# A graph-attention kernel: in the last pass, every fourth step sums A (E - 1) g into the bank of the A f products

## The chip, the cores and the metric

The kernel runs on one core of one Trainium2 chip. The metric is the device time of one execution in microseconds (us); the time of a version is the median of its runs.

## The reference, cut to what matters

Two layers work on 4096 nodes with 512 features. Layer 0 is graph attention with 8 heads of width 64, followed by a residual sum and a layer norm. Layer 1 is attention inside graphs of 128 nodes, again with residual and layer norm.

```python
# layer 0, per head h; A is the 4096 x 4096 adjacency of zeros and ones
feats   = einsum('nf,hfo->hno', X, W)
dense   = s_self[:, :, None] + s_neigh[:, None, :]
dense   = where(dense > 0, dense, 0.2 * dense) * A    # a missing edge counts with exp(0) = 1
out     = softmax(dense) @ feats ; relu ; x = layernorm(x + out)
# layer 1
scores  = (x Wq^T)(x Wk^T)^T * scale + 2 adj, inside blocks of 128 ; off-block scores are -1e6 * (2 adj)
x       = layernorm(x + (softmax(scores) * mask) @ (x Wv^T))
```

A missing edge has the weight 1 and an edge the weight E = exp(leaky(s + t)), where s belongs to the row's node and t to the neighbour. So a row of layer 0 is the sum of all f (S), plus the sum over edges of (E - 1) f, divided by the sum of the weights.

## The kernel before, in words

**How E is taken apart.** With p = exp(0.8 s), u = exp(-0.2 s), d = exp(-0.8 t) and g = exp(t) f, the product u E f is max(p, d) g. So u times the wanted sum is u (S - A f) + A max(p, d) g. The kernel keeps two PSUM accumulators of two banks each: `accf` sums -A f and `acc` sums A max(p, d) g. At the end of a chunk `sums_to_rows` forms `y = (accf + S) * u_row + acc` (L1259 and L1267).

**Tiling.** A pass r (0 to 3) treats two heads. A pass has four chunks c of 1024 target nodes, and a chunk has 32 steps j of 128 neighbours. For one step VectorE makes two tiles of 128 x 1024 called `q`, one per head (L1475): `q = max(p_row, d) * A`. ScalarE turns q into a `mark` of zeros and ones for the denominators (L1485); of each fourth step, the second head's mark is made on VectorE (L1480). TensorE does 4 matmuls `accf` with the adjacency tile `at` and the two halves of f (L1499), and 8 matmuls `acc` with q and g (L1521), each on 32 columns; in the trace each of the 8 appears as two. Every eight steps the `dens` matmuls sum the marks (L1536).

**Order of the work.** In the last pass four steps form a group, so a chunk has the groups g0 to g7. TensorE runs in the order of the program: in a group 16 accf, then pieces of other work, then 32 acc (64 in the trace), then further pieces. The other engines are ordered by the framework's scheduler. In the last pass the pool of q tiles has 6 buffers, that is three steps: the q of a fourth step can be written only when acc of the first step of its group has been read. `at` has 6 buffers too, and is loaded on the SP queue.

**The pieces.** In the chunks c1, c2 and c3 of the last pass, the lists `PLAN` and `PLANS` put layer 1 of the preceding chunk between the main matmuls. A chunk is two blocks of layer 1, "a" and "b". "E" closes the preceding chunk: transposes of the denominators and of `y` into three PSUM tiles `ps_m` (L1316, L1339), and on VectorE `parts`, `rd` (L1319 to L1332) and two multiplications `hst` (L1340), which free the PSUM tiles. Then `rows_of_layer_0` makes the rows `x1b` (L1246), and a layer norm follows. The pieces a and b transpose x1b (L1075), make scores (L1095, L1122, L1131), values (L1167, L1175) and output rows (L1181, L1183). In c1, block b does not exist yet; in c2 and c3, block b of the chunk before is finished in g0 to g2. All these pieces take their PSUM tiles from the same three buffers in turn (`misc`).

**The setup** ends with the rows of exponentials: `exponentials` writes p and u of 128 nodes to `pu_j` (L744), `rows_of_exponentials` transposes them on TensorE (L768), copies them on ScalarE (L777) and stores them to the DRAM tensor `pu_d`, from which p_row and u_row are later loaded as broadcast rows (L1412, L1418).

Of the kernel before, what the change touches and what calls it, by code (L numbers as in the profile page):

```python
# [404 lines left out]
def adjacency_streamed_path(  # L405
# [55 lines left out]

    g_d = dram.tile([PR, NT // 4, P, 4 * FP], F32, name="g_d")
    f_d = dram.tile([PR, NT // 4, P, 4 * 2 * FP], F32, name="f_d")
    pu_d = dram.tile([2 * H, N], F32, name="pu_d")
    at_d = dram.tile([NCH, NT, P, C], F32, name="at_d")
    hs_d = dram.tile([N, FP * (PR - 1)], F32, name="hs_d")

# [25 lines left out]
    p_all, u_all = pu_all[:, :, 0, :], pu_all[:, :, 1, :]  # L493
    n0 = const.tile([P, NT], F32, name="n0")
    nb_all = const.tile([P, NT, H], F32, name="nb_all")
    e_all = early.tile([P, NT, 2, H], F32, name="e_all")
    e_b = const.tile([P, NT, H, 6], BF16, name="e_b")

# [36 lines left out]
    urowp = ctx.enter_context(tc.tile_pool(name="urows", bufs=1))  # L535
    evp = ctx.enter_context(tc.tile_pool(name="ev", bufs=1))
    hp_ = ctx.enter_context(tc.tile_pool(name="hout", bufs=1))
    ckp = ctx.enter_context(tc.tile_pool(name="ck", bufs=2))
    ps0 = ctx.enter_context(tc.tile_pool(name="ps_misc", bufs=1, space=PSUM))
    banks = [ps0]  # L540

# [90 lines left out]
    with tc.tile_pool(name="setup1", bufs=1, side="right") as one, tc.tile_pool(  # L632
# [97 lines left out]
        def exponentials(k, u, sc):  # L730

            j = 4 * k + u
            if u == 0:
                pu_js[k] = two.tile([P, 4, 2, H], F32, name="pu_j")
            st = small.tile([P, 5, H], F32, name="st")
            for lo, hi, w in ((0, 3, 1), (3, 5, 0)):
                ends_of_setup["DVE", u] = nc.vector.tensor_tensor(
                    st[:, lo:hi].rearrange("p k (q h) -> p k q h", q=2),
                    sc[:, None, :, :, w].to_broadcast([P, hi - lo, 2, H // 2]),
                    powers[:, lo:hi].rearrange("p k (q h) -> p k q h", q=2),  # L740
                    OP.mult,
                )
            nc.scalar.activation(e_all[:, j], st[:, 0:2], AF.Exp)
            nc.scalar.activation(pu_js[k][:, u], st[:, 3:5], AF.Exp)  # L744
            nc.scalar.activation(d_all[:, j, :], st[:, 2], AF.Exp)

        def parts_of_exponentials(k):
            blk = slice(4 * k, 4 * k + 4)
            nc.vector.tensor_scalar_mul(
                nb_all[:, blk, :], d_all[:, blk, :], -BIG * (1.0 + 2.0**-23)  # L750
            )
            eb = e_b[:, blk]
            for i in range(2):
                src = e_all[:, blk, i, :]
                rest = small.tile([P, 4, H], F32, name="rest")
                nc.vector.tensor_copy(eb[:, :, :, 3 * i], src)
                nc.vector.tensor_sub(rest, src, eb[:, :, :, 3 * i])
                nc.vector.tensor_copy(eb[:, :, :, 3 * i + 1], rest)
                nc.vector.tensor_sub(eb[:, :, :, 3 * i + 2], rest, eb[:, :, :, 3 * i + 1])
            nc.vector.tensor_copy(  # L760
                e_p[:, blk, :NE].rearrange("p j (m h) -> p j h m", h=H), eb[:, :, :, :3]
            )
            nc.vector.tensor_scalar_mul(eb[:, :, :, :3], eb[:, :, :, :3], -1.0)

        def rows_of_exponentials(k):
            pr = pss.tile([2 * H, 4, P], F32, name="ps_set")
            for u in range(4):
                nc.tensor.transpose(  # L768
                    pr[:, u, :], pu_js[k][:, u].rearrange("p k h -> p (k h)"), ident
                )  # L770
            if k < NB - 1:
                row = late.tile([2 * H, 4 * P], F32, name="pu_row")
            else:
                row = hp_.tile([P, CT, FP], F32, name="hst")
                row = row.rearrange("p t n -> p (t n)")[: 2 * H, : 4 * P]
            rows[k] = row
            ends_of_setup["ROW"] = nc.scalar.copy(  # L777
                row.rearrange("p (q n k) -> p q k n", q=2, k=2),
                pr.rearrange("p (q k) n -> p q k n", q=2),
            )  # L780
            nc.gpsimd.dma_start(pu_d[:, ts(k, 4 * P)], row)

        def columns_of_exponentials(k, pc=None):
            pc = pss.tile([P, 4, 2 * H], F32, name="ps_set") if pc is None else pc
            for u in range(4):
                nc.tensor.transpose(pc[:, u, :], rows[k][:, ts(u, P)], ident[: 2 * H, : 2 * H])
            nc.vector.tensor_copy(
                pu_all[:, 4 * k : 4 * k + 4].rearrange("p u k h -> p u (k h)"), pc
            )
# [138 lines left out]
    def columns_of_last():  # L928

        columns_of_exponentials(NB - 1, misc([P, 4, 2 * H]))  # L930

    psa = ctx.enter_context(tc.tile_pool(name="ps_acc_f", bufs=1, space=PSUM))
    dens = psa.tile([P, HB], F32, name="dens")
    nc.vector.memset(dens, 0.0)
# [134 lines left out]
    def layer_1(blk, x1b, lp, lp1, lp2):  # L1069
# [45 lines left out]
            if c % 2:  # L1115
                yield
        pq = misc([P, 4, P])
        ns = lp1.tile([P, 4, P], F32, name="ns")
        nm = small.tile([P, 4], F32, name="nm_f")
        for u in range(4):  # L1120
            for f in range(FC):
# [72 lines left out]
        pp = misc([P, 4, P])  # L1194
        for u in range(4):
            nc.tensor.transpose(pp[:, u, :], ns[:, u, :], ident)
        pT = lp1.tile([P, 4, P], F32, name="pT_f")
        nc.scalar.copy(pT, pp)
        values(1)
        yield  # L1200
# [49 lines left out]
    def sums_to_rows(r, c, acc, accf, ae, u_row, later_by):  # L1250
# [25 lines left out]
        def pieces():  # L1276
# [55 lines left out]
            nc.vector.reciprocal(rd, rd)  # L1332
            if r == 0:
                yield later_by
            hst = hp_.tile([P, CT, FP], F32, name="hst")
            for t4 in range(0, CT, 4):
                fin = misc([P, 4, FP])
                for t in range(4):
# [65 lines left out]
    def main_pass(r, ae=None, wide=4):  # L1404

        for c in range(NCH):
# [8 lines left out]
            for h in range(2):  # L1415
                in_order(
                    r == 0 and c < 2,
                    nc.sync.dma_start(  # L1418
                        u_row[h * FH : (h + 1) * FH, :],
                        broadcast_rows(pu_d[H + 2 * r + h, ts(c, C)], FH, C),  # L1420
                    ),
                )
            def pieces(c, group, place):
                if r == PR - 1 and c:
                    run_plan(PLANS[c == NCH - 1][group][place])
                elif place == (r == 0):
                    run_pieces((0.75 if r else 1.0) * wide)
# [18 lines left out]
            for j0 in range(0, NT, wide):  # L1446
# [13 lines left out]
                    in_order(r == 0 and c == 0 and j0 < 16, ins)  # L1460
                if at_step == 0:
                    cast_steps(0, 6, last_pair)
                follow = [
                    x
                    for x in steps[at_step + wide : at_step + 2 * wide]
# [3 lines left out]
                for j in cycle:  # L1469
                    for h in range(2):  # L1470
                        hh = 2 * r + h
                        q = qs[j, h] = ring("q", qp, 6).tile([P, C], F32, name="q")
                        d_j = d_all[:, j, hh : hh + 1]
                        with following(at_step == 0, ("DVE", 3 if j else 2)):
                            ends_of_setup["Q"] = nc.vector.scalar_tensor_tensor(  # L1475
                                q, p_row[h], d_j, ats[r, c, j].bitcast(F32), op0=OP.max, op1=OP.mult
                            )
# [16 lines left out]
                    with following(True, "Q"):  # L1494
                        parts_of_exponentials(NT // 4 - 1)
                for j in cycle:
                    for w in range(2):
                        for s in range(2):
                            nc.tensor.matmul(  # L1499
                                accf[:, s, :],  # L1500
                                f_s[j // 4][:, j % 4, w, :],
                                ats[r, c, j][:, ts(s, HB)],
                                start=(j == 0 and w == 0),
                                stop=(j == NT - 1 and w == 1),
                            )
# [9 lines left out]
                    pieces(c, j0 // 4, 0)  # L1515

                for j in cycle:
                    for s in range(2):
                        for o in range(0, FP, 32):
                            h = o // FH  # L1520
                            nc.tensor.matmul(  # L1521
                                acc[o : o + 32, s, :],
                                g_s[j // 4][:, j % 4, h, o % FH : o % FH + 32],
                                qs[j, h][:, ts(s, HB)],
                                start=(j == 0),
                                stop=(j == NT - 1),
                            )
                if r == 0:
                    pieces(c, j0 // 4, 1)
# [117 lines left out]
```

## Time and profile before

| | us |
|---|---|
| median of 3 runs | 2055.48 (2055.07 to 2056.7) |
| profiled execution | 2057.91, its span 2056.1 |
| chunks c0, c1, c2, c3 of the last pass, from the first accf matmul of each | 1354.1, 1450.8, 1604.8, 1775.3 |
| last acc matmul of the last pass ends | 1931.9 |

The profiled execution is one of its own; its time lies 2.4 us above the median of the runs. In the profile PE is TensorE, PEld its weight loads, DVE VectorE, ACT ScalarE, POOL GpSimd and SP the queue that issues most loads. "busy" of TensorE is modelled: a busy TensorE can still be held up by a late operand. In a line of a group, the shapes follow as output and input, then the count, the busy time in us and the mean in ns, and behind the bar the idle time before it and who ended it.

### The profile page before, as it was taken

How to read it: one execution, taken by the hardware profiler on the slowest of the kernel's cores; microseconds unless marked ns; L12 is line 12 of the kernel's file. 1: busy time of each engine (PE TensorE's matmuls, PEld its weight loads, DVE VectorE, ACT ScalarE, POOL GpSimd, SP SyncE). 2: the span in 40 equal slices, each digit the busy share in tenths (PEclk: the TensorE clock that was granted, in tenths of full speed). 3: DMA queues.
4: the chain of work that ended last, by engine and by line, in shares of the span. 5: the costliest groups of instructions: out<-in, count | busy, mean ns of one | idle time of the engine just before them, and what ended most of it. 6: DMA issues, size and time to landing. Idle time of an engine off the chain costs nothing.

```text
span 2056.1 us, 38302 instructions
## 1 busy us (share of the span) xinstructions
PE 2030.4 (99%) x15105; PEld 1051.0 (51%) x15105; DVE 1671.9 (81%) x2125; ACT 1542.2 (75%) x1878; POOL 224.2 (11%) x361
## 2 busy tenths in 40 slices
PE   9999999999999999999999999999999999999997
PEld 7884555555544444444454444544454445545453
DVE  5668888888899998798998999999975984896654
ACT  3349888888879889788898989998885666567420
POOL 1222222222100000000000000000210210210111
PEclk9999999999999999999999999999999999999999
DMA  6999999999999999798999999989974764775211
GB/s 208 245 325 259 287 288 276 291 268 289 271 373 337 354 352 335 257 310 298 319 323 340 316 336 323 326 295 358 323 237 144 250 242 137 225 274 169 73 49 43
DMA packets 207371, 551.31 MB, mean 268 GB/s; under 512 B 24780, under 2 KB 65740, under 8 KB 207180
## 3 DMA queue, kind: packets, MB, share of 16 engines
q1 hardware_dynamic: 142828, 426.31, 59.6%
q0 software_dynamic: 62272, 121.91, 23.2%
q8 instruction: 121, 1.98, 0.4%
q10 hardware_dynamic: 2080, 0.52, 0.1%
q14 instruction: 70, 0.57, 0.1%
HBM read 491.79 MB, written 107.22 MB: 291 GB/s over the span
## 4 chain that ended last, share of the span: by engine, by line
PE 93%; DVE 4%; issue 1%; DMA 1%; SPq 0%; POOL 0%; ACT 0%; POOLq 0%; DVEq 0%
PE acc L1521 41%; PE accf L1499 23%; PE ps_fe L800 5%; PE ps_m L1167 5%; PE dens L1536 5%; PE ps_m L1095 5%; DVE q L1475 3%; PE ps_m L1122 1%; PE ps_m L610 1%; PE ps_m L1181 1%; PE ps_m L1075 1%; PE ps_m L1024 1%; PE ps_m L1339 1%; PE ps_set L720 1%; PE ae L1435 1%
## 5 line engine op out<-in xcount | busy, mean ns | idle before, releaser
L1475 DVE SCALAR_TENSOR_TENSOR q<-p_row,d_all,at 128x1024 f32<-128x1024 f32 x1024 | 1242.0, 1277 | 146.9 <-PE acc L1521 121.1
L1485 ACT ACTIVATE mark<-q,nb_all 128x1024 fp8e4<-128x1024 f32 x896 | 995.5, 1145 | 184.3 <-DVE q L1475 168.6
L1521 PE MATMUL acc<-q,g_s 128*32 128x512 f32 x8192 | 903.4, 593 | 1.1 <-DVE q L1475 0.4
L1521 PEld LDWEIGHTS acc<-q,g_s 128*32 128x32 f32 x8192 | 264.1, 110 | 594.4 <-issue 533.0
L1499 PE MATMUL accf<-at,f_s 128*128 128x512 f32 x2048 | 495.2, 398 | 2.1 <-ACT at L621 2.1
L1499 PEld LDWEIGHTS accf<-at,f_s 128*128 128x128 f32 x2048 | 380.3, 188 | 110.4 <-issue 26.4
L1230 ACT ACTIVATE ck<-ck,neg_half_f 128x1024 f32<-128x1024 f32 x128 | 146.0, 1141 | 25.5 <-DMA ck<-in_adj_dram 25.4
L1231 ACT ACTIVATE ck<-ck,neg_quarter 128x1024 f32<-128x1024 f32 x128 | 146.3, 1143 | 1.7
L1536 PE MATMUL dens<-mark,e_b 128*6 128x512 fp8e4 x2048 | 125.3, 379 | 0.0
L800 PE MATMUL ps_fe<-w_sb_f,xT_f 128*128 128x264 f32 (+1 forms) x512 | 121.1, 393 | 1.9 <-ACT xT_f L723 1.9
L621 ACT CAST at<-ps_m 128x1024 fp32r<-128x1024 fp8e4 x124 | 116.4, 1025 | 4.8 <-PE ps_m L610 4.3
L1167 PE MATMUL ps_m<-wvT,x1T 128*128 128x512 f32 x256 | 114.2, 594 | 0.0
L1095 PE MATMUL ps_m<-x1T,M_sb 128*128 128x512 f32 x256 | 112.9, 594 | 0.0
L800 PEld LDWEIGHTS ps_fe<-w_sb_f,xT_f 128*128 128x128 f32 x512 | 100.1, 199 | 16.4 <-ACT xT_f L723 2.5
L1350 POOL DMA_DIRECT2D hs_d<-hst x12 | 10.7, 896 | 847.8 <-DVE hst L1340 847.8
L1480 DVE TENSOR_SCALAR mark<-q,d_all 128x1024 fp8e4<-128x1024 f32 x128 | 96.3, 752 | 4.7
L622 POOL DMA_DIRECT2D at_d<-at x128 | 69.0, 541 | 272.3 <-ACT at L621 248.1
L1536 PEld LDWEIGHTS <-e_b 128*6 128x6 bf16 x2048 | 54.7, 86 | 77.7 <-issue 34.6
L1095 PEld LDWEIGHTS ps_m<-x1T,M_sb 128*128 128x128 f32 x256 | 48.0, 190 | 59.3 <-issue 58.4
L1167 PEld LDWEIGHTS ps_m<-wvT,x1T 128*128 128x128 f32 x256 | 47.6, 190 | 56.4 <-issue 55.2
L1175 DVE TENSOR_TENSOR v_t<-ps_m,bv_row 128x512 f32<-128x512 f32 x32 | 21.7, 684 | 60.5 <-PE ps_m L1167 60.5
L1102 ACT ACTIVATE zT<-ps_m,zb 128x512 f32<-128x512 f32 x32 | 21.7, 680 | 61.2 <-PE ps_m L1095 61.2
(195 smaller groups left out, 1099.5 us busy)
## 6 DMA issues: line engine op xcount, KB each, us to landing
at<-at_d SPq DMA_DIRECT2D x384, 512.0 KB, 6.3
f_s<-f_d SPq DMA_DIRECT2D x128, 512.0 KB, 7.8
at_d<-at POOLq DMA_DIRECT2D x128, 512.0 KB, 14.8
ck<-in_adj_dram SPq DMA_DIRECT2D x128, 512.0 KB, 5.5
g_s<-g_d SPq DMA_DIRECT2D x128, 256.0 KB, 5.6
f_d<-fst POOLq DMA_DIRECT2D x16, 1024.0 KB, 7.9
a_b<-in_adj_dram POOLq DMA_DIRECT2D x32, 512.0 KB, 17.4
p_row<-pu_d SPq DMA_DIRECT2D x32, 512.0 KB, 6.9
```

Source lines behind the costliest of these rows:

```text
L621: ends_of_setup["ACT"] = nc.scalar.copy(at, both[:, :, k])
L800: nc.tensor.matmul(pf[:, q, :, cols], tile_j(xTs[k][:, c].rearrange("p u n -> p (u n)"), u), w_sb[:, c, 4 * q : 4 * q + 4, cols], start=(c ...
L1095: nc.tensor.matmul(pz, L1["M"][:, f, ts(c, P)], x1T[:, f, :], start=(f == 0), stop=(f == FC - 1),)
L1167: nc.tensor.matmul(pv, x1T[:, f, ts(u, P)], L1["wvT"][:, f, :], start=(f == 0), stop=(f == FC - 1),)
L1230: tc.keep_in_program_order(nc.scalar.activation(ck, ck, AF.Square, bias=neg_half))
L1231: nc.scalar.activation(ck, ck, AF.Abs, bias=neg_quarter, accum_out=binp[:, k : k + 1])
L1475: ends_of_setup["Q"] = nc.vector.scalar_tensor_tensor(q, p_row[h], d_j, ats[r, c, j].bitcast(F32), op0=OP.max, op1=OP.mult)
L1480: nc.vector.tensor_scalar(mark, q, d_j, None, op0=OP.is_gt, saturate=False)
L1485: nc.scalar.activation(mark, q, AF.Sigmoid, bias=nb_all[:, j, hh : hh + 1], scale=BIG, saturate=False,)
L1499: nc.tensor.matmul(accf[:, s, :], f_s[j // 4][:, j % 4, w, :], ats[r, c, j][:, ts(s, HB)], start=(j == 0 and w == 0), stop=(j == NT - 1 an ...
L1521: nc.tensor.matmul(acc[o : o + 32, s, :], g_s[j // 4][:, j % 4, h, o % FH : o % FH + 32], qs[j, h][:, ts(s, HB)], start=(j == 0), stop=(j ...
L1536: nc.tensor.matmul(dens[lo : lo + 6, :], e_b[:, j, 2 * r + h, :], marks[j, h][:, ts(s, HB)], start=(j == 0), stop=(j == NT - 1),)
```

## The change

In chunks c1, c2 and c3 of the last pass, the steps j = 2, 6, ..., 26 are folded: one step in each of the groups g0 to g6, 21 steps in all. A folded step has no accf matmuls. Its q is made by two VectorE instructions per head in place of one, `max(p_row, d) * U_row` and then `(q - c) * A`, with U = 1/u as a broadcast row and c = exp(-t) as a column. So q g is A (E - 1) f, and its 8 matmuls add to accf in place of acc. Its mark is made on ScalarE from the sign of q, with a constant bias (a folded step never is the one whose mark VectorE makes).

To have U and c, the setup takes reciprocals: eight of 128 x 8 for c, and eight of 128 x 8 for U ahead of the transposes of `pu_j`, which have 18 rows in place of 16. Each of the three chunks loads two rows of U (512 KB each in SBUF). They lie in the buffers `hst` and `U_row`. For that, the last pass forms hst in place in y, and layer 1 keeps its scores `ns` and their transposes `pT` in the tile a4, where before each had a tile of its own. The pool `ck` is opened later.

```diff
+            def folded(j):
+                if r == PR - 1:
+                    return r in FOLDED and c > 0 and j % 4 == 2 and j < NT - 4
...
+                    row = pool.tile(shape, F32, name=name)
+                    U_row.append(row.rearrange("p t n -> p (t n)") if len(shape) == 3 else row)
+                    nc.sync.dma_start(
+                        U_row[h],
+                        broadcast_rows(pu_d[2 * H + 2 * FOLDED.index(r) + h, ts(c, C)], P, C),
+                    )
...
+                if not U_row and any(folded(j) for j in cycle):
+                    rows_for_folded()
...
+                        if folded(j):
+                            cn = c_all[r][:, j, h : h + 1]
+                            nc.vector.scalar_tensor_tensor(
+                                q, p_row[h], d_j, U_row[h], op0=OP.max, op1=OP.mult
+                            )
+                            nc.vector.scalar_tensor_tensor(
+                                q, q, cn, ats[r, c, j].bitcast(F32), op0=OP.subtract, op1=OP.mult
+                            )
+                            mark = marks[j, h] = sgp.tile([P, C], FP8, name="mark")
+                            nc.scalar.activation(
+                                mark, q, AF.Sigmoid, bias=below_0, scale=2.0**80, saturate=False
+                            )
+                            continue
...
-                    for w in range(2):
+                    for w in range(0 if folded(j) else 2):
...
+                    dst = accf if folded(j) else acc
...
-                                acc[o : o + 32, s, :],
+                                dst[o : o + 32, s, :],
...
+            for r in FOLDED:
+                nc.vector.reciprocal(
+                    c_all[r][:, blk], e_all[:, blk, 1, 2 * r : 2 * r + 2]
+                )
...
+            for i, r in enumerate(FOLDED):
+                nc.vector.reciprocal(
+                    pu_js[k][:, :, 2 * H + 2 * i : 2 * H + 2 * i + 2],
+                    pu_js[k][:, :, H + 2 * r : H + 2 * r + 2],
+                )
...
-            hst = hp_.tile([P, CT, FP], F32, name="hst")
+            if r == PR - 1:
+                hst = y.rearrange("p (t n) -> p t n", t=CT)
+            else:
+                hst = hp_.tile([P, CT, FP], F32, name="hst")
...
-        ns = lp1.tile([P, 4, P], F32, name="ns")
+        ns = a4
...
-        pT = lp1.tile([P, 4, P], F32, name="pT_f")
+        pT = a4
```

In the built program the scheduler also places other instructions anew. On VectorE, in g0 of c1, c2 and c3, the four instructions of the folded step stand where `parts`, `rd` and the first `hst` stood; these follow now behind the last q of g0, and both `hst` multiplications behind the first two q of g1. At the end of the setup, ScalarE's copy of the last exponential rows (L777) stands behind two casts of `at` in place of one.

More of the change, by code (lines that the diff above doesn't have):

```diff
@@ L463, in adjacency_streamed_path @@
     f_d = dram.tile([PR, NT // 4, P, 4 * 2 * FP], F32, name="f_d")
-    pu_d = dram.tile([2 * H, N], F32, name="pu_d")
+    FOLDED = (PR - 1,)
+    HU = 2 * len(FOLDED)
+    pu_d = dram.tile([2 * H + HU, N], F32, name="pu_d")
     at_d = dram.tile([NCH, NT, P, C], F32, name="at_d")
@@ L495, in adjacency_streamed_path @@
     nb_all = const.tile([P, NT, H], F32, name="nb_all")
+    c_all = {
+        r: (const if r else early).tile([P, NT, 2], F32, name="c_all") for r in FOLDED
+    }
+    below_0 = const.tile([P, 1], F32, name="below_0")
+    nc.gpsimd.memset(below_0, -128.0)
     e_all = early.tile([P, NT, 2, H], F32, name="e_all")
@@ L537, in adjacency_streamed_path @@
     hp_ = ctx.enter_context(tc.tile_pool(name="hout", bufs=1))
-    ckp = ctx.enter_context(tc.tile_pool(name="ck", bufs=2))
     ps0 = ctx.enter_context(tc.tile_pool(name="ps_misc", bufs=1, space=PSUM))
@@ L733, in exponentials @@
             if u == 0:
-                pu_js[k] = two.tile([P, 4, 2, H], F32, name="pu_j")
+                pu_js[k] = two.tile([P, 4, 2 * H + HU], F32, name="pu_j")
             st = small.tile([P, 5, H], F32, name="st")
@@ L743, in exponentials @@
             nc.scalar.activation(e_all[:, j], st[:, 0:2], AF.Exp)
-            nc.scalar.activation(pu_js[k][:, u], st[:, 3:5], AF.Exp)
+            nc.scalar.activation(
+                pu_js[k][:, u, : 2 * H].rearrange("p (k h) -> p k h", k=2), st[:, 3:5], AF.Exp
+            )
             nc.scalar.activation(d_all[:, j, :], st[:, 2], AF.Exp)
@@ L765, in rows_of_exponentials @@
         def rows_of_exponentials(k):
-            pr = pss.tile([2 * H, 4, P], F32, name="ps_set")
+            for i, r in enumerate(FOLDED):
[3 more added lines that the diff above has]
+                )
+            pr = pss.tile([2 * H + HU, 4, P], F32, name="ps_set")
             for u in range(4):
-                nc.tensor.transpose(
-                    pr[:, u, :], pu_js[k][:, u].rearrange("p k h -> p (k h)"), ident
-                )
+                nc.tensor.transpose(pr[:, u, :], pu_js[k][:, u], ident)
             if k < NB - 1:
-                row = late.tile([2 * H, 4 * P], F32, name="pu_row")
+                row = late.tile([2 * H + HU, 4 * P], F32, name="pu_row")
             else:
                 row = hp_.tile([P, CT, FP], F32, name="hst")
-                row = row.rearrange("p t n -> p (t n)")[: 2 * H, : 4 * P]
+                row = row.rearrange("p t n -> p (t n)")[: 2 * H + HU, : 4 * P]
             rows[k] = row
@@ L785, in columns_of_exponentials @@
             for u in range(4):
-                nc.tensor.transpose(pc[:, u, :], rows[k][:, ts(u, P)], ident[: 2 * H, : 2 * H])
+                nc.tensor.transpose(
+                    pc[:, u, :], rows[k][: 2 * H, ts(u, P)], ident[: 2 * H, : 2 * H]
+                )
             nc.vector.tensor_copy(
@@ L930, in columns_of_last @@
         columns_of_exponentials(NB - 1, misc([P, 4, 2 * H]))
+    ckp = ctx.enter_context(tc.tile_pool(name="ck", bufs=2))
     psa = ctx.enter_context(tc.tile_pool(name="ps_acc_f", bufs=1, space=PSUM))
@@ L1422, in main_pass, with rows_for_folded @@
                 )
+            U_row = []
+            def folded(j):
+                if r == PR - 1:
+                    return r in FOLDED and c > 0 and j % 4 == 2 and j < NT - 4
+                return r in FOLDED and j % 8 == 6 and (0 if c else 8) < j < NT - 8
+            def rows_for_folded():
+                for h in range(2):
+                    if r == PR - 1:
+                        pool, shape, name = ((hp_, [P, CT, FP], "hst"), (pools.get("lp1"), [P, C], "U_row"))[h]
+                    else:
+                        pool, shape, name = ckp, [P, CK], "ck"
+                    row = pool.tile(shape, F32, name=name)
[4 more added lines that the diff above has]
+                    )
             def pieces(c, group, place):
@@ L1473, in main_pass @@
                         d_j = d_all[:, j, hh : hh + 1]
+                        if folded(j):
[5 more added lines that the diff above has]
+                                q, q, cn, ats[r, c, j].bitcast(F32), op0=OP.subtract, op1=OP.mult
+                            )
+                            mark = marks[j, h] = sgp.tile([P, C], FP8, name="mark")
+                            nc.scalar.activation(
+                                mark, q, AF.Sigmoid, bias=below_0, scale=2.0**80, saturate=False
+                            )
+                            continue
                         with following(at_step == 0, ("DVE", 3 if j else 2)):
@@ L1526, in main_pass @@
                                 stop=(j == NT - 1),
+                                skip_group_check=folded(j),
                             )
```

## The prediction

> **What bounds the kernel now.** I read the engine shares first, then the costliest groups, then the last pass cut into its groups of four steps, and last the order of single instructions where two engines are both full. The first two, in the page of the kernel before:
>
> ```profile
> PE 2030.4 (99%) x15105; PEld 1051.0 (51%) x15105; DVE 1671.9 (81%) x2125; ACT 1542.2 (75%) x1878; POOL 224.2 (11%) x361
> ...
> L1475 DVE SCALAR_TENSOR_TENSOR q<-p_row,d_all,at 128x1024 f32<-128x1024 f32 x1024 | 1242.0, 1277 | 146.9 <-PE acc L1521 121.1
> L1521 PE MATMUL acc<-q,g_s 128*32 128x512 f32 x8192 | 903.4, 593 | 1.1 <-DVE q L1475 0.4
> L1499 PE MATMUL accf<-at,f_s 128*128 128x512 f32 x2048 | 495.2, 398 | 2.1 <-ACT at L621 2.1
> ```
>
> TensorE has hardly any idle time and q is the largest work of VectorE; q waits mostly for acc to give a buffer back. So over the whole span TensorE sets the time. The 81% of VectorE is an average, and the change acts in one pass only. There the stretches of c1 (about g0, g1, and g4 to g6) and of c2 (about g0, g1, g3, and g4 to g6) read, with the columns stretch, length, then busy time and count of TensorE, its weight loads, VectorE, ScalarE and GpSimd, the clock and the DMA:
>
> ```profile
> 1450.80:1463.40 12.60, 12.60 (x94) 6.40 (x92) 12.37 (x22) 10.57 (x12) 0.00 (x0) 1.00 0.96 337
> 1463.40:1478.80 15.40, 14.97 (x114) 5.97 (x112) 15.40 (x22) 11.37 (x20) 4.00 (x3) 1.00 0.96 335
> ...
> 1510.60:1553.00 42.40, 42.40 (x274) 22.04 (x273) 27.12 (x40) 34.73 (x47) 1.91 (x6) 1.00 0.55 180
> 1604.80:1625.60 20.80, 20.45 (x116) 9.65 (x113) 20.63 (x37) 10.95 (x17) 5.09 (x6) 1.00 0.79 275
> 1625.60:1646.80 21.20, 21.20 (x135) 9.64 (x133) 20.29 (x26) 16.79 (x19) 2.62 (x4) 1.00 0.71 236
> ...
> 1660.50:1681.00 20.50, 20.50 (x139) 10.35 (x138) 19.18 (x35) 13.63 (x17) 4.14 (x5) 1.00 0.91 343
> 1681.00:1723.50 42.50, 42.50 (x275) 22.14 (x273) 31.12 (x44) 33.82 (x45) 2.21 (x6) 1.00 0.48 155
> ```
>
> The reader is to see two regimes. From g4 on, VectorE is busy for 27 to 31 of 42 us: there is room. In g0 to g3 both engines are full (20.63 of 20.80, 15.40 of 15.40): there VectorE has no room for anything.
>
> **What the Trainium skill says.** "Perfetto Trace Analysis", Identifying the Most-Contended Engine, warns that the busy share of matmuls does not measure nearness to the limit; its Optimization Strategy says that the most contended engine may change between regimes. The stretches agree: TensorE's 99% hides that VectorE is level with it in g0 to g3. "VectorE: DVE Perf Modes", The DRAIN you can't avoid, says that a read after a write on VectorE itself needs a semaphore. The second fold instruction reads what the first wrote; the built order is mostly first(h0), first(h1), second(h0), second(h1), so another instruction stands between. No row of before shows such a wait: 0 in most groups, 0.7 us in g1 of c1, where the four are spread, as an estimate. The section Matmuls of the first page wants matmul groups to rotate through PSUM banks, so that the emptying of one overlaps the next; here these are the three `ps_m` tiles, and it matters below when they are emptied late.
>
> **The change part by part.** *TensorE, removed.* Sixteen accf at the head of a group take 4.24 us in g1 of c2 (3.92 in g0); start to start in an undisturbed run they are 229 ns apart. A folded step drops four: 0.92 us, and 21 steps 19.2 us. The 64 acc of a group (7.1 us) stay; some only change their bank.
>
> *VectorE, added.* Two more instructions of q's size per folded step. Price from the row above: 1277 ns busy; in runs of q the starts are 1.195 us apart. (The skill, "VectorE: DVE Perf Modes", The TRN2 errata, gives (N+151)/0.96 ns for an fp32 add of two tensors, an estimate of 1.22 us at 1024: within 5%.) So 2 x 1.195 = 2.39 us a step, and 50.2 us in all. Per group the change trades 0.92 us of TensorE for 2.39 us of VectorE.
>
> *Which of them counts.* q has six buffers, three steps. The last q of a group waits for the acc of the group's first step, so VectorE cannot run ahead into the next group: a group lasts as long as the longer of TensorE's work and VectorE's work between the last q's of two neighbouring groups. I added the latter from the order of VectorE's instructions in both programs, by their spacings. In us, group length before / VectorE before / VectorE after:
>
> - c1: g0 14.3/13.7/13.7, g1 13.7/13.8/18.1, g2 12.6/12.0/14.4, g3 12.6/12.7/12.6.
> - c2 and c3: g0 15.5/14.8/15.0, g1 19.9/19.9/21.2, g2 21.2/16.0/19.2, g3 13.0/13.0/16.2.
> - all three: g4 26.3/21.2/25.3 (c1: 19.0 before), g5 16.1/11.4/13.8, g6 33.6/11.5/13.9 (c3: 26.8 long).
>
> Against each, TensorE needs 0.92 less than before. In g4 to g6 it stays the longer: 3 x -0.92 = -2.8 a chunk. In c1 g0 to g3 give 13.7 - 14.3, 18.1 - 13.7, 14.4 - 12.6 and 0: +5.6, with the spread fold +6.3; with g4 to g6 c1 is +3.6. In c2 and c3 they give -0.5, +1.3, -0.9, +3.2 = +3.1, and with g4 to g6 +0.3.
>
> *VectorE, moved.* In c2 and c3 comes a wait. Before, VectorE's and TensorE's orders there are, with start, length and engine first:
>
> ```profile
> 1613.62 0.69 DVE L1340 TENSOR_TENSOR hst<-ps_m,rd 128x512 f32<-128x512 f32 x1
> ...
> 1621.62 0.66 DVE L1340 TENSOR_TENSOR hst<-ps_m,rd 128x512 f32<-128x512 f32 x1
> ...
> 1618.60 3.70 PE L1167 MATMUL ps_m<-wvT,x1T 128*128 128x512 f32 x8
> 1622.13 0.60 PE L1196 MATMUL ps_m<-ident_f,ns 128*128 128x128 f32 x4
> 1622.57 3.60 PE L1167 MATMUL ps_m<-wvT,x1T 128*128 128x512 f32 x8
> ```
>
> Both `hst` run before they are needed, or nearly. In the changed order `parts` and the two `hst` stand behind q of g0's last step and the first two q of g1. The three tiles they empty are those that the values, the transposes of ns and the second values take. By the spacings, TensorE waits there about 0.5 and 3.7 us, with the second values, and behind them the accf of g1, queued. VectorE in turn stands at `v_t` (L1175), which reads these values. Then g1 needs 19.0 + 4.2 = 23.2 instead of 21.2: +2.0 in each chunk, +2.3 with the above. `hst` late makes x1b (L1246) late, and with it the buffer of the third load `hp_l`, which lands 4 to 5 us after it is let go; c2's g4 then finds its rows late. Bounds 0 and 2.4 us; I take 1.5. So +3.8 for c2 and for c3.
>
> *Setup.* Before:
>
> ```profile
> 155.08 0.60 PE L768 MATMUL ps_set<-ident_f,pu_j 128*16 128x128 f32 x4
> ...
> 156.23 0.59 ACT L777 COPY hst<-ps_set 16x512 f32<-16x512 f32 x1
> ...
> 157.77 1.53 PE L1499 MATMUL accf<-at,f_s 128*128 128x512 f32 x4 [2.09 <-ACT at L621]
> ```
>
> The last transposes now wait for a reciprocal behind a 0.67 us multiplication, and the copy stands behind one more cast of 1.0 us. The first accf waits for the end of these: +1.0 (0 to 1.5), and TensorE, full from there on, never makes it up. The other fifteen reciprocals are 0.2 us each where VectorE is busy 56 to 68%: 0.
>
> *DMA and buffers.* Six loads of 512 KB for U. The program issues c1's during c0, the others after the previous chunk's folded steps are over, 45 us or more ahead, where the DMA share is about 0.5; p_row's equal loads land in 6.9 us. Cover gone, each 0 to 3 us; I take 0. On SP they stand ahead of `at`, whose loads have some 10 us to spare. The loads into a4 wait for the last use of pT, but are still early: 0, and if late they would hold x1T's transposes. ScalarE's mark reads q as before, 1145 ns: 0.
>
> **Sum.** 3.6 + 3.8 + 3.8 + 1.0 = +12.2. The profiled execution (2057.91, span 2056.1) becomes 2070.1. It lay 2.4 above the median, so the median becomes 2055.5 + 12.2, about 2068.
>
> **Rivals.** *A, the longer engine only:* the late `hst` is hidden, because TensorE comes later to its pieces as well. Then c1 gives +2.9, c2 and c3 +0.3 each, setup +1.0: +4.5, 2060. For it: TensorE really is held back by VectorE at just these places. Against it: the order of VectorE is fixed in the program, and three tiles are few.
>
> *B, the other side, faster:* VectorE's additions are covered everywhere, because the three steps of q in store carry over the full groups. Then 19.2 - 1.0 = 18.2 is gained: 2037. The place is g0 to g3 and the price 12 x 2.39 = 28.7 us of VectorE; it decides once VectorE has about that much free in those groups. Their stretches show less than 3 us free in c1's g0 and g1 or c2's g0 and g1; what speaks for it is only g2 of c2 (16.0 of 21.2).
>
> *C, VectorE sets all of g0 to g3:* every added VectorE us counts there: 28.7 - 9 x 0.92 + 1.0 = +21.4, 2077, and up to 2082 with late x1b. For it: the 15.40 of 15.40. Against: g2 has room.
>
> That the change does nothing is excluded by the built order: 84 accf are gone and 84 VectorE instructions are there.
>
> **How the numbers follow.** Chances: my sum 0.55, A 0.20, C 0.13, B 0.07, others (a load late, or an exact balance) 0.05. Two runs of this kernel can be told apart from about 0.2%, 4.1 us. A reaches into that band with some 0.08; B gives faster, with one hundredth from the rest; slower has 0.83. My sum's own range is 2064 to 2073 (setup 0 to 1.5, x1b 0 to 2.4 twice, spread fold). With A's lower half and C's upper edge it is 2058 to 2080.
>
> **What would show it.** Right: VectorE near 100% in g0 to g3 of c1 to c3; its total up by about 50 us; accf x1964; in c2 and c3 TensorE idle at L1167's or L1196's tiles for `hst`; the first accf at 158.8; c1 from 154.0 to 157.6, c2 from 170.5 to 174.3; g4 to g6 shorter by 0.9 each. Wrong: q with idle time from U's loads; no wait for `hst` (A); g0 to g3 no longer than before (B); g4 no shorter (C).

## The result, and the profile after

The change made the kernel slower by 0.7%: 2070.47 us median (2063.02 to 2072.47, 6 runs) against 2055.28 us (6 runs, the three named above among them); the ratio is 1.0069, with a 95% interval of 1.0049 to 1.0088. The forecast was 2068, 12.2 us more; the medians differ by 15.2. The profiled execution of the changed kernel took 2072.47 us, its span is 2070.7; before it was 2057.91 and 2056.1. So the two profiles lie 14.6 us apart and can be compared part by part.

The engine shares and the costliest groups of the changed kernel, from its page:

```profile
PE 2030.7 (98%) x15021; PEld 1039.4 (50%) x15021; DVE 1719.2 (83%) x2183; ACT 1540.5 (74%) x1876; POOL 237.0 (11%) x362
...
L1533 DVE SCALAR_TENSOR_TENSOR q<-p_row,d_all,at 128x1024 f32<-128x1024 f32 x982 | 1192.8, 1277 | 131.6 <-PE acc L1580 122.1
...
L1557 PE MATMUL accf<-at,f_s 128*128 128x512 f32 x1964 | 477.0, 399 | 1.7 <-ACT at L627 1.7
```

The counts are as the diff says: 84 accf fewer, and 42 plain q fewer. Their place is taken by 84 others, by shape and line, from the groups in the last three chunks:

```profile
L1524 DVE SCALAR_TENSOR_TENSOR q<-q,c_all,at 128x1024 f32<-128x1024 f32 x42 | 51.9, 1274 | 0.0
L1580 PE MATMUL accf<-q,g_s 128*32 128x512 f32 x336 | 50.0, 633 | 10.3 <-DVE q L1524 9.6
...
L1521 DVE SCALAR_TENSOR_TENSOR q<-p_row,d_all,U_row 128x1024 f32<-128x1024 f32 x21 | 26.8, 1274 | 0.0
L1521 DVE SCALAR_TENSOR_TENSOR q<-p_row,d_all,hst 128x1024 f32<-128x1024 f32 x21 | 26.7, 1271 | 0.0
```

A fold instruction costs what a plain q costs, 1.27 us. VectorE's busy time rose by 47.3 us (the busy times count overlaps once). The matmuls that sum q into accf stand idle for 10.3 us, 9.6 of it for the second fold instruction (6.2 in g1 of c1, 1.7 in g3 of c2 and of c3); before, in these chunks, TensorE had waited for q for 0.4 us in all. In TensorE's waits in the last three chunks, with total, count and the longest, one sees what is new:

```profile
PE accf L1580 <- DVE q L1524: 9.6, 4, 4.5
PE ps_m L1214 <- DVE ys L1361: 2.5, 2, 1.7
PE acc L1580 <- DVE q L1533: 1.5, 2, 0.9
PE ps_m L1185 <- ACT a L1216: 1.3, 2, 0.7
```

The second line is the wait for the late `hst` multiplication (named `ys` now, since it is formed in y). The last is of the same place: the second values wait for the copy of the transposes.

The stages by their first accf matmul, with the difference to before:

| | before | after | difference |
|---|---|---|---|
| first accf of the kernel | 157.8 | 159.9 | +2.1 |
| c0 of the last pass | 1354.1 | 1355.1 | +1.1 |
| c1 | 1450.8 | 1451.0 | +0.2 |
| c2 | 1604.8 | 1608.8 | +3.9 |
| c3 | 1775.3 | 1783.2 | +7.9 |
| last acc ends | 1931.9 | 1945.7 | +13.8 |
| span | 2056.1 | 2070.7 | +14.6 |

Cut into groups, from first accf to first accf, the differences are: c1 -0.6, +7.0, -0.9, 0, +0.1, -0.9, -0.9, 0; c2 +1.7, -0.1, -0.9, +5.1, +0.2, -0.9, -0.9, 0; c3 +4.2, -0.1, -0.9, +5.4, then -0.9 three times, 0. (Pieces that stand behind the acc of g0, the values among them, fall into g0 here.) In c0 nothing is folded; its -0.9 lies in the fourth group, and the run without any fold (below) has it too.

The stretches that answer to those shown of before, of c1 (g0, g1, g4 and g5) and of c2 (g0, g1, g3, g4 and g5), columns as there:

```profile
1451.00:1463.00 12.00, 12.00 (x90) 5.94 (x88) 12.00 (x13) 10.78 (x12) 0.00 (x0) 1.00 0.93 321
1463.00:1485.40 22.40, 16.15 (x111) 5.43 (x109) 22.40 (x37) 13.86 (x30) 5.61 (x5) 0.77 0.89 305
...
1516.20:1557.90 41.70, 41.70 (x267) 20.76 (x265) 39.48 (x53) 36.39 (x48) 6.28 (x9) 1.00 0.59 189
...
1608.80:1631.20 22.40, 20.63 (x113) 8.77 (x109) 22.00 (x38) 14.16 (x20) 2.83 (x4) 1.00 0.75 252
1631.20:1652.20 21.00, 21.00 (x129) 9.36 (x128) 20.00 (x27) 12.19 (x15) 3.70 (x6) 1.00 0.74 238
...
1665.10:1690.60 25.50, 22.27 (x133) 8.86 (x132) 21.87 (x41) 15.82 (x26) 3.46 (x8) 1.00 0.82 283
1690.60:1732.40 41.80, 41.77 (x267) 20.79 (x265) 39.89 (x53) 32.96 (x42) 4.13 (x8) 1.00 0.52 166
```

In g1 of c1 VectorE is busy for all of 22.40 us and TensorE for 16.15. In g4 and g5 VectorE went from 27 and 31 us to about 40 of 42, and yet the stretches became 0.7 to 0.8 us shorter. (The stretches that the prediction labels "g4 to g6", 42.4 and 42.5 us long, hold g4 and g5 only; its numbers by group are not touched by that.)

The orders around the late `hst` in c2, of VectorE and then of TensorE, from the timeline:

```profile
1617.94 2.47 DVE L1533 SCALAR_TENSOR_TENSOR q<-p_row,d_all,at 128x1024 f32<-128x1024 f32 x2
1620.33 0.20 DVE L1337 TENSOR_REDUCE parts<-ps_m 128x16 f32<-128x48 f32 x1
...
1625.45 0.56 DVE L1264 SCALAR_TENSOR_TENSOR x1b<-hp_l,x1b 128x384 f32<-128x384 f32 x1 [0.40 <-DMA hp_l<-hs_d]
1625.93 0.68 DVE L1361 TENSOR_TENSOR ys<-ps_m,rd 128x512 f32<-128x512 f32 x1
```

```profile
1622.31 3.70 PE L1185 MATMUL ps_m<-wvT,x1T 128*128 128x512 f32 x8
1626.76 0.63 PE L1214 MATMUL ps_m<-ident_f,a 128*128 128x128 f32 x4 [0.75 <-DVE ys L1361]
1628.06 3.70 PE L1185 MATMUL ps_m<-wvT,x1T 128*128 128x512 f32 x8 [0.68 <-ACT a L1216]
```

`parts` follows the four fold instructions and the last q of g0, the first `hst` comes 12.3 us later than before (1625.93 against 1613.62, in a chunk that began 3.9 later), and TensorE's transposes wait for it. In c3 the load of x1b's rows, hp_l, held VectorE for 1.39 us where in c2 it was 0.40, and TensorE waited 1.74 and 0.67.

The setup, from the timeline:

```profile
157.23 0.19 DVE L779 RECIPROCAL pu_j<-pu_j 128x8 f32<-128x8 f32 x1
...
157.57 0.60 PE L785 MATMUL ps_set<-ident_f,pu_j 128*18 128x128 f32 x4 [1.15 <-DVE pu_j L779]
158.31 0.60 ACT L792 COPY hst<-ps_set 18x512 f32<-18x512 f32 x1
...
159.85 2.50 PE L1557 MATMUL accf<-at,f_s 128*128 128x512 f32 x5 [1.69 <-ACT at L627]
```

The transposes wait 1.15 us for the reciprocal. The copy ends 2.1 us later than in the profile of before, of which 1.2 lies ahead of this place already. Counted from the same cast of `at` (it starts at 155.14 here, at 153.97 before), the first accf comes after 4.71 us here and after 3.80 before: 0.9 us more. But this is made up at once: by the same count the 33rd accf, 29 us further on, comes 0.2 us earlier than before.

### The profile page after: what moved, and what is told of

It is laid out like the page before. It is cut to its first block, busy times and chain, and to the rows that moved or that the text cites. A ratio compares the mean times of both kernels' runs of the same rounds, so it can differ in the third digit from the quotient of the medians.

```text
span 2070.7 us, 38211 instructions
## 1 busy us (share of the span) xinstructions
PE 2030.7 (98%) x15021; PEld 1039.4 (50%) x15021; DVE 1719.2 (83%) x2183; ACT 1540.5 (74%) x1876; POOL 237.0 (11%) x362
## 4 chain that ended last, share of the span: by engine, by line
PE 89%; DVE 5%; DMA 2%; issue 1%; ACT 1%; POOL 0%; SPq 0%; POOLq 0%; DVEq 0%; ACTq 0%
PE acc L1580 38%; PE accf L1557 22%; PE ps_fe L817 6%; PE ps_m L1185 5%; PE dens L1596 5%; PE ps_m L1113 4%; DVE q L1533 3%; PE accf L1580 2%; PE ps_m L616 1%; PE ps_m L1140 1%; PE ps_m L1199 1%; DMA hp_l<-hs_d 1%; PE ps_set L726 1%; PE ps_m L1042 1%; PE ps_m L1093 1%
## 5 line engine op out<-in xcount | busy, mean ns | idle before, releaser
L1533 DVE SCALAR_TENSOR_TENSOR q<-p_row,d_all,at 128x1024 f32<-128x1024 f32 x982 | 1192.8, 1277 | 131.6 <-PE acc L1580 122.1
L1543 ACT ACTIVATE mark<-q,nb_all 128x1024 fp8e4<-128x1024 f32 x854 | 949.5, 1145 | 166.5 <-DVE q L1533 151.1
L1580 PE MATMUL acc<-q,g_s 128*32 128x512 f32 x7856 | 879.0, 594 | 2.3 <-DVE q L1533 1.5
L1580 PEld LDWEIGHTS acc<-q,g_s 128*32 128x32 f32 x7856 | 254.2, 110 | 574.6 <-issue 505.7
L1557 PE MATMUL accf<-at,f_s 128*128 128x512 f32 x1964 | 477.0, 399 | 1.7 <-ACT at L627 1.7
L1557 PEld LDWEIGHTS accf<-at,f_s 128*128 128x128 f32 x1964 | 365.1, 189 | 107.0 <-issue 26.8
L1248 ACT ACTIVATE ck<-ck,neg_half_f 128x1024 f32<-128x1024 f32 x128 | 146.0, 1140 | 28.8 <-DMA ck<-in_adj_dram 28.7
L1528 ACT ACTIVATE mark<-q,below 128x1024 fp8e4<-128x1024 f32 x42 | 47.2, 1144 | 23.0 <-DVE q L1524 22.5
```

Source lines behind the costliest of these rows:

```text
L1248: tc.keep_in_program_order(nc.scalar.activation(ck, ck, AF.Square, bias=neg_half))
L1533: ends_of_setup["Q"] = nc.vector.scalar_tensor_tensor(q, p_row[h], d_j, ats[r, c, j].bitcast(F32), op0=OP.max, op1=OP.mult)
L1543: nc.scalar.activation(mark, q, AF.Sigmoid, bias=nb_all[:, j, hh : hh + 1], scale=BIG, saturate=False,)
L1557: nc.tensor.matmul(accf[:, s, :], f_s[j // 4][:, j % 4, w, :], ats[r, c, j][:, ts(s, HB)], start=(j == 0 and w == 0), stop=(j == NT - 1 an ...
L1580: nc.tensor.matmul(dst[o : o + 32, s, :], g_s[j // 4][:, j % 4, h, o % FH : o % FH + 32], qs[j, h][:, ts(s, HB)], start=(j == 0), stop=(j ...
```

## The experiments

**Late and early folds.** The first question was whether the gain and the loss lie where the two regimes put them. Each run changes the one line that says which steps are folded.

```diff
-                    return r in FOLDED and c > 0 and j % 4 == 2 and j < NT - 4
+                    return r in FOLDED and c > 0 and j % 4 == 2 and NT // 2 < j < NT - 4
```

> Folded only at j = 18, 22, 26 of c1 to c3, where VectorE has room (groups g4 to g6). My theory, that a group lasts as long as the longer of its two engines: 9 x -0.92 = -8.3 us, setup +1.0, so about -7 against the kernel before, 2048; no lengthening of g0 to g3; if g4 gains nothing, as in the changed kernel, 3 x 0.92 less of it, about -4.5. Rival, that each fold costs its 2.39 us of VectorE wherever it stands, since the scheduler's order lets nothing be hidden: 9 x (2.39 - 0.92) + 1.0 = +14, 2070.

Measured: 2049.76 (2046.69 to 2052.76), ratio 0.9973 (0.9963 to 0.9983). In its profile every one of the nine groups is 0.9 us shorter, and no other is longer by more than 0.4; TensorE waits for q for 0.8 us in all. So where VectorE has room, two more instructions of 1.2 us cost nothing, and 0.9 us a fold is the gain. Of the nine gains, 8.2 us, the median shows 5.6, as the rest of the change costs 0.8 to 3.5 (see the run without folds). The rival is out by 20 us.

```diff
-                    return r in FOLDED and c > 0 and j % 4 == 2 and j < NT - 4
+                    return r in FOLDED and c > 0 and j % 4 == 2 and j < NT // 2
```

> Folded only at j = 2, 6, 10, 14 of c1 to c3, where both engines are full (g0 to g3). My theory: all of the loss lies here, so the changed kernel without the gain of g4 to g6: 2070.5 + 5.5 to 8.3, 2076 to 2079. Rival (the cost is spread evenly): less than the changed kernel, 12 of 21 of its +15, +8.7, 2064.

Measured: 2074.22 (2071.91 to 2081.02), ratio 1.0092 (1.0078 to 1.0105). That is 3.8 us over the changed kernel, less than the 5.5 to 8.3 expected, and the intervals of the two ratios overlap; the rival's 2064 is out. In its profile (of the slowest of its five runs) c1 to c3 are 18.6 us longer than before, against 13.6 with all 21 folds. So the loss lies with the twelve early folds, and the nine late ones take some of it back.

**Everything but the folds.**

```diff
-                    return r in FOLDED and c > 0 and j % 4 == 2 and j < NT - 4
+                    return False
```

> No step is folded and no U is loaded; the reciprocals, the 18 rows and the new places of hst, ns, pT and ck stay. My theory: the setup's wait alone, +1.0 us (first accf at about 159.9, +1.0 left by c1 of the first pass), and nothing from the buffers: 2055 to 2057. Rival, that the shared tile a4 or hst in y costs something in the last pass: the chunks c1 to c3 longer by 1 us or more each, 2059 or more.

Measured: 2057.61 (21 runs), ratio 1.0010 (1.0004 to 1.0017), so 0.8 to 3.5 us. In its profile c1, c2 and c3 start 0.1, 0.1 and 0.4 us later than before and the last acc ends 0.5 later. So the shared tile a4 and hst in y cost nothing in the last pass. Where the 0.8 to 3.5 us come from is not shown. The copy stands behind two casts here too, and from the cast named above to the first accf it takes 4.71 us, as in the changed kernel; but of these 0.9 us only 0.2 are left 29 us later. What lies ahead of that cast can't be had from the profiles: the first accf was at 157.4 to 160.8 us in those of kernels with this same setup, and the granted clock of the first 40 us differs among them.

**One step fewer, so that hst comes early.** In c2 and c3 j = 2 is not folded; the scheduler then leaves parts, rd and hst where they were before.

```diff
-                    return r in FOLDED and c > 0 and j % 4 == 2 and j < NT - 4
+                    return r in FOLDED and c > 0 and j % 4 == 2 and (0 if c == 1 else 4) <= j < NT - 4
```

> As the changed kernel, but the step j = 2 of c2 and c3 is not folded (in c1 it is), so that parts, rd and the first hst stand in g0 as before. My theory: TensorE no longer waits for hst at the transposes in g1; c2 and c3 lose about 2.0 + 1.3 us less each (g1 18.9 of VectorE in place of 21.2, g3 14.3 in place of 16.2, g2 21.2 in place of 20.3): about -3 to -5 a chunk, 2061 to 2065. Rival, that the wait for hst is only where VectorE's lateness shows, and not a cost of its own: one fold less saves 2.39 - 0.92 = 1.5 a chunk, 2067.5.

Measured: 2061.85 (2060.79 to 2064.64), ratio 1.0035 (1.0023 to 1.0047): 8.6 us less than the changed kernel for two folds fewer. TensorE's waits in the last three chunks are now only these:

```profile
PE accf L1580 <- DVE q L1524: 9.4, 4, 4.6
PE acc L1580 <- DVE q L1533: 1.5, 6, 0.4
```

The waits for the second fold instruction are nearly the same; both waits at the transposes and the values are gone. c2 is +0.9 and c3 -0.6 against before, in place of +4.0 and +5.8, and g3 alone +2.2 in both, in place of +5.1 and +5.4. So a fold in g0 cost 3.1 and 6.4 us there by the profiles, 4.3 by the medians, where its VectorE time less its accf would be 1.5: the late hst is a cost of its own. (The run takes the fold and the late order away together; the old order with the fold kept was not run.)

**Each half of the exchange alone.** First TensorE's: a folded step keeps its place in accf, but its q is the plain one, so that U and c are missing from the sum.

```diff
-                            nc.vector.scalar_tensor_tensor(
-                                q, p_row[h], d_j, U_row[h], op0=OP.max, op1=OP.mult
-                            )
-                            nc.vector.scalar_tensor_tensor(
-                                q, q, cn, ats[r, c, j].bitcast(F32), op0=OP.subtract, op1=OP.mult
-                            )
+                            nc.vector.scalar_tensor_tensor(
+                                q, p_row[h], d_j, ats[r, c, j].bitcast(F32), op0=OP.max, op1=OP.mult
+                            )
```

> The changed kernel with the plain single q in the folded steps: the 84 accf are left out, no VectorE instruction is added (the sum lacks U and c there, so what is computed is not the reference). My theory, by the longer of the two engines with VectorE's order of this kernel: c1 -4.4, c2 and c3 -5.7 each, setup +0.8: -15, 2040. Rival, that dropping accf gives little, because TensorE's time is set elsewhere (only g4 to g6 gain): -8.3 + 0.8, 2048.

Measured: 2045.26 (2043.77 to 2048.98), ratio 0.9958 (0.9943 to 0.9974), -9.5 us: nearer the rival's 2048 than my 2040. The chunks are 3.9 to 4.1 us shorter. g4 to g6 give their 2.7 to 2.8; g0 to g3 give 1.2 to 1.4 where four dropped accf in each are 3.7. So even with no VectorE instruction added, two thirds of TensorE's saving in g0 to g3 is not to be had. That VectorE was level there already, more than my table of groups said, fits this, but was not separated: hst stands later in VectorE's order here too (in c2 it starts 15.7 us after the chunk does, before 8.8), and g1 is 0.6 to 0.7 us longer in all three chunks.

Then VectorE's, in the kernel before: q of the same 21 steps is written twice.

```diff
+                        if r == PR - 1 and c > 0 and j % 4 == 2 and j < NT - 4:
+                            nc.vector.scalar_tensor_tensor(
+                                q, p_row[h], d_j, ats[r, c, j].bitcast(F32), op0=OP.max, op1=OP.mult
+                            )
                         with following(at_step == 0, ("DVE", 3 if j else 2)):
```

> The kernel before with each q of the 21 steps written twice by VectorE: its additional 42 instructions alone, all accf kept, setup and buffers as before. My theory: g4 to g6 hide theirs; g0 to g3 grow by +6.2 in c1 and by +4.5 (if hst stays early) to +8 (if it falls behind as in the changed kernel) in c2 and c3: +15 to +22, 2071 to 2077. Rival, that VectorE's additions are covered and the loss comes from the folds' other parts (the sign mark, U's loads, the bank): 2056.

Measured: 2069.54 (2068.69 to 2071.94), ratio 1.0071 (1.0056 to 1.0087), +14.7 us. Its chunks are +5.9, +5.6 and +5.0, all in g0 to g4. TensorE's waits in the last three chunks:

```profile
PE acc L1525 <- DVE q L1479: 5.9, 3, 4.6
PE ps_m L1167 <- ACT pT_f L1198: 1.3, 2, 0.7
PE ps_m L1196 <- DVE hst L1340: 1.3, 2, 0.7
```

The stop for q and the waits for the late hst are here again, without a load of U or a folded sum. The 42 VectorE instructions alone, without any other part of the change, are enough for the measured loss. A lowered TensorE clock, which the last section describes, can't be the cause: in these chunks the granted clock was lowered only once, to 0.50 from 1474.3 to 1481.1, so at most half of 6.8 us, of 16.5, comes of it (an estimate). The two halves don't add up to the whole (-9.5 + 14.7 = +5.2 against +15.2). About 3.9 of the 10 us between are the savings of g0 to g3 that no longer count once VectorE sets these groups (3 x 1.3); the rest wasn't split further.

**What makes g1 of c1 so long.** It is the largest single difference (+7.0). The four fold instructions of j = 6 are spread there, with the layer norm's statistics between; my prediction had put 0.7 us on that.

```diff
-                    return r in FOLDED and c > 0 and j % 4 == 2 and j < NT - 4
+                    return r in FOLDED and c > 0 and j % 4 == 2 and j < NT - 4 and (c, j) != (1, 6)
```

> The changed kernel without the fold at j = 6 of c1, where the four instructions stand spread, with x1b and its layer norm's statistics between the first and the second. My theory: of the +6.5 us of that group, what the spread and the additional VectorE work cost goes (15.7 of VectorE by its order in place of 18.1, and no half-made q in between), and the clock after TensorE's stop of 4.5 us stays at full: 2.4 to 5 us less than the changed kernel, 2065.5 to 2068. Rival, that the group is late because parts, rd and hst moved into it from g0: only 2.4 - 0.9 = 1.5 us less, 2069.

Measured: 2069.3 (2064.48 to 2070.78), ratio 1.0061 (1.0047 to 1.0075), 1.2 us under the changed kernel, at the rival's value, though the two intervals overlap. Then the block moved from g0 was suspected instead, and j = 2 of c1 left out:

```diff
-                    return r in FOLDED and c > 0 and j % 4 == 2 and j < NT - 4
+                    return r in FOLDED and c > 0 and j % 4 == 2 and j < NT - 4 and (c, j) != (1, 2)
```

> The changed kernel without the fold at j = 2 of c1; j = 6 of c1 stays folded. In the built order parts, rd, hst, x1b and the statistics of c1 then stand where they stood before, ahead of the last q of g0 and of g1, and g1's fold stands together behind them. Theory formed from the run without j = 6: the group g1 of c1 is late because that block is moved behind the four q of g1; from the first accf of g0 to that of g3 the changed kernel took 6.0 us more than before, and without j = 6 still 4.7. If so, this run takes clearly less than 4.7 there, 2.4 (one fold's VectorE work in g1) + 1.8 (g2) - 0.9 = 3.3 or less. Rival: each fold of g0 to g2 costs the same wherever it stands: 4.5 to 4.7.

Measured: 2068.22 (2064.14 to 2070.07), ratio 1.0065 (1.0052 to 1.0079). The 6.0 and 4.7 us in this expectation are in truth counted from the first accf of g1 to that of g3. So counted, this run takes 4.3 more than before; from g0's to g3's the three stand at +5.5, +4.1 and +4.2. So 4.3 lies nearer the rival's 4.5 than the 3.3 of the theory, and the moved block is not the cause either: either fold left out saves about 1.3 us, near 2.39 - 0.92 = 1.47. The clock was full in all of c1 in this run. In c1, g0 to g2 act as one stretch that VectorE fills, and a fold there costs its VectorE time less its accf, wherever it stands. The stop of 4.5 us is only where that shows.

**Folding where there is room.** If a group's slack decides, more can be folded late than the change does. One step of g5, three of g6 and one of g7 were taken; U comes from ScalarE as an exponential, so that the transposes don't wait for VectorE.

```diff
-                    return r in FOLDED and c > 0 and j % 4 == 2 and j < NT - 4
+                    return r in FOLDED and c > 0 and j in (22, 24, 25, 26, 30)
...
+            for i, r in enumerate(FOLDED):
+                nc.scalar.activation(
+                    pu_js[k][:, u, 2 * H + 2 * i : 2 * H + 2 * i + 2],
+                    st[:, 4, 2 * r : 2 * r + 2],
+                    AF.Exp,
+                    scale=-1.0,
+                )
...
-                nc.vector.reciprocal(
-                    pu_js[k][:, :, 2 * H + 2 * i : 2 * H + 2 * i + 2],
-                    pu_js[k][:, :, H + 2 * r : H + 2 * r + 2],
-                )
```

> Folded where VectorE has room: j = 22, 24, 25, 26, 30 of c1 to c3 (one step of g5, three of g6, one of g7), and U by ScalarE as exp of the negated exponent in place of the reciprocal, so that the copy of the last rows keeps its place ahead of the second cast. My theory: 15 x -0.92 = -13.8, setup at most +0.3, VectorE's order in g1 of c2 and c3 up to +1 each: 2041.5 to 2044. Rival, that three folds in a row hold VectorE up (7.2 us more at once, with three steps of q in store): g6 gains nothing, 2050.

Measured: 2046.74 (2044.33 to 2049.44), ratio 0.9960 (0.9946 to 0.9973), -8.1 in place of -11 to -14. g6 gave its 2.7 us in all three chunks, so three folds in a row are covered. The step in g7 took 0.6 us in c1 and in c2 where it should have given 0.9 (in c3 it gave 0.4): the sum that empties accf came late for the next chunk,

```profile
1599.02 3.93 PE L1559 MATMUL accf<-at,f_s 128*128 128x512 f32 x16 [0.93 <-DVE ys L1279]
```

and g1 of c2 and of c3 became 1.2 and 1.5 us longer, as VectorE's order there had moved. The next one adds j = 18 and 27, and j = 10 in c2 and c3:

```diff
-                    return r in FOLDED and c > 0 and j in (22, 24, 25, 26, 30)
+                    return r in FOLDED and c > 0 and (j in (18, 22, 24, 25, 26, 27, 30) or (c > 1 and j == 10))
```

> As the one above, with j = 18 and 27 of c1 to c3 and j = 10 of c2 and c3 folded too: 23 steps. My theory: 23 x -0.92 = -21.2, with the same +0.3 and up to +1 twice: 2034 to 2036. Rival, that g2 and g4, where VectorE would have 18.9 of 20.3 and 23.6 of 25.4 us, are too full: as the one above or slower, 2042 or more.

Measured: 2046.89 (2045.3 to 2047.77), ratio 0.9964 (0.9950 to 0.9977): eight folds more and no gain. g4 gave its 0.9 us in each chunk. But g5 and g6 together gave 2.8 in each chunk where five folds should give 4.6. A group with all four steps folded has no accf left at its head, so that its first q is wanted at once; that this is the reason was not tried by itself. g2 of c2 and c3 gave nothing.

So the last one keeps j = 18, 22, 24, 25 and 26, with U as in the two before:

```diff
-                    return r in FOLDED and c > 0 and j in (22, 24, 25, 26, 30)
+                    return r in FOLDED and c > 0 and j in (18, 22, 24, 25, 26)
```

> Folded at j = 18, 22, 24, 25, 26 of c1 to c3 (one step of g4, one of g5, three of g6, none of g7), U by ScalarE's exp. My theory: in the run with j = 30 folded it was this step that stood in VectorE's order ahead of the sum that empties accf, and made the next chunk's first accf wait 0.93 us, and moved hst in g1; without it nothing is given back: 15 x -0.92 = -13.8, setup 0 to +0.5: 2041 to 2042. Rival, that the three folds of g6 make VectorE late for g7 whatever g7 holds: about -8 as with j = 30, 2046.5.

Measured: 2040.44 (2040.15 to 2045.52), ratio 0.9931 (0.9917 to 0.9945). It beats both kernels, by 14.6 and by 30 us. In its profile g4, g5 and g6 are shorter by 0.9, 0.9 and 2.7 in c1 (c2 and c3 within 0.1 of that), no other group from c1 on differs by more than 0.1, and TensorE's waits in the last three chunks are these:

```profile
PE acc L1582 <- DVE q L1535: 0.4, 2, 0.2
```

## Why the prediction was right

The direction and the size were right, and so was the main place, g0 to g3. The sum was 3 us short of the medians (12.2 against 15.2) and 2.4 short of the two profiles (14.6). That it came so near is in part luck. The three chunks were put at 11.2 us and took 13.6. The 1.0 of the setup was made up before the last pass, and c1 begins only 0.2 later than before; behind the last acc there are 0.8 that no term stands for.

- *Two regimes, and the longer engine.* Shown: 0.9 us gained in each late fold by itself, a loss with the early ones, and VectorE's additions alone enough for the loss. The prices held: 0.9 us measured for the accf, and 4.79 us for the four instructions of a fold in g0 of c2 (1613.15 to 1617.94), so 2.39 for two. The rule failed for the accf alone: it gave -15 us, and -9.5 were measured.
- *c1:* +3.8, predicted +3.6 (its terms, 6.3 - 2.8, make 3.5). Two errors offset each other: g0 to g3 grew by 5.5 where 6.3 stood, and g4 gave nothing where 0.9 stood. The 0.7 us for the spread fold has no support, since leaving that fold out saved what leaving out another one did.
- *c2:* +4.0, predicted +3.8. *Late hst* is supported by the run that puts it early, but it was mis-sized: TensorE's waits were 0.75 and 0.68 us, not 0.5 and 3.7, and x1b's late rows acted there, ahead of hst in VectorE's queue (0.40 us), not at g4. In its place g3 grew by 5.1 us where the table had 3.2; with hst early it grew by 2.2. So VectorE's lateness was carried on and came out in g3.
- *c3:* +5.8, predicted +3.8. Its g0 grew by 2.5 us more than that of c2. Two terms that the sum did not have are as large together: hp_l's load held hst for another 1.0 us, and TensorE took the second values in 5.26 us in place of 3.70 while its clock was lowered (1.6). That they make up the 2.5 is a sum of durations, not a test. The clock was lowered in g3 too (3.92 us for the folded step in place of 2.68), but g3 is only 0.3 us over that of c2.
- *g4:* 0.9 gained was predicted in each chunk. It came in c3 only (+0.1 in c1, +0.2 in c2). With late folds alone it came in all three. The table had put VectorE at 25.3 of TensorE's 25.4 us there, too near to be counted as a gain.
- *Setup:* the place was right, 0.9 us at the first accf against +1.0. That TensorE never makes it up was wrong: 29 us later it is gone. Everything but the folds still cost 0.8 to 3.5 by the medians; where, is open.
- *DMA and the shared buffers at 0:* right. U's loads ended no wait of VectorE; the run without folds shows a4 and y to be free.
- *Rival A* (2060) is out: the late hst is not hidden, and without it, with two folds fewer, the time is 2061.85. *Rival B* (2037) is out as a forecast for this change, but its cover holds where VectorE has room, and the last kernel uses it there. *Rival C* (2077) is out as a whole: it put g0 to g3 at +28.7 us, and they grew by 19.7; g2 became 0.9 shorter in each chunk. But its sign, g4 no shorter, came in c1 and c2.

## What to carry to other kernels

An exchange of one engine's work for another's is priced by stage, not by the shares of the whole span: the same edit gained 0.9 us in a group where VectorE was busy for two thirds to three quarters of the time, and cost 1.3 to 4.3 us where it was level with TensorE. Where slack is found, put as much of the exchange there as it holds, and none in the stages beside it. And look in the built order at what the added instructions push back: a small instruction that empties a PSUM tile cost more when late (4.3 - 1.5 = 2.8 us a fold, by the medians) than the added work itself.

## What the runs showed of the hardware that was not expected

The granted TensorE clock drops after TensorE has stood still. In the changed kernel the 5 us after the stop of 4.5 us in c1, the next 5 us, the 5 us with the 1.68 us stop in g3 of c2, and those of the stops in c3 read, with the clock third from the end:

```profile
1475.00:1480.00 5.00, 3.27 (x16) 0.60 (x16) 5.00 (x6) 2.68 (x14) 3.41 (x3) 0.50 1.07 330
1480.00:1485.00 5.00, 5.00 (x50) 1.51 (x44) 5.00 (x8) 5.00 (x10) 1.10 (x3) 0.76 0.59 194
1676.00:1681.00 5.00, 3.79 (x28) 0.88 (x32) 5.00 (x6) 4.18 (x5) 0.00 (x0) 1.00 0.65 246
1800.00:1805.00 5.00, 2.58 (x8) 1.26 (x7) 4.09 (x11) 2.63 (x4) 0.00 (x0) 0.83 0.40 126
1805.00:1810.00 5.00, 5.00 (x13) 2.56 (x12) 3.35 (x9) 0.79 (x2) 1.28 (x2) 0.83 0.36 105
```

The Trainium skill ("TensorE: Matmul & The Clock Gate", Part 1) says that the clock falls to half after an idle window of about 3.4 us. The level agrees, 0.50 here. The time does not. The stop in c1 begins at 1469.65; the share is 1.00 until 1472.20 and 0.50 from there on, so it fell 2.55 us into the stop. The two stops of 1.74 and 0.67 us in c3 were followed by a drop too (0.50 from 1803.3 to 1806.7). Of two stops of 1.68 us, in g3 of c3 and in g3 of c2, the first was followed by one (0.50 from 1854.5 to 1857.9) and the second was not. So in this trace the length of one stop does not decide alone. The mean clock differs from run to run of the changed kernel: 0.994 and 0.996 in its two quickest (2063.02, 2064.45), 0.990 to 0.993 in the other four (2070.33 to 2072.47). That the drops cause this spread is argued from that, not shown.
